# Mirrored rows of W: by a matmul with a flipped identity, or by a gather and sums on GpSimd

## The chip, the core and the metric

The kernel runs on one core of a Trainium2 chip. A core has five engines that work in parallel, each through its own instructions in their order: TensorE (PE: matrix products into PSUM), VectorE (DVE), ScalarE (ACT), GpSimd (POOL, which doesn't reach PSUM) and SyncE (SP, which here only issues DMAs). They wait for each other through semaphores. The metric is the device time of one execution in microseconds, lower is better.

## The reference

A transformer block with cross-attention and a Fourier layer, all in float32: `x` is (2, 2048, 512), the context (2, 128, 512).

```python
q = layernorm(x) @ wq + bq;  k = ctx @ wk + bk;  v = ctx @ wv + bv     # 16 heads of 32
score = (q . k) / sqrt(32) * mask;  score = where(score == 0, -1e9, score)
x = x + softmax(score) @ v @ wo + bo
w = complex(w_freq_real, w_freq_imag)                                  # (512, 512)
x = x + real(ifft(fft(layernorm(x)) @ w)) + bias
```

The Fourier layer is linear, so it equals `layernorm(x) @ M` with one real matrix M of 512x512. The kernel computes M once, on the chip, from the two halves of w and a table of cosines and sines. By symmetry the product needs only sums and differences of mirrored rows (row j of w with row 512 - j), then of mirrored columns.

## The kernel before

The 4096 rows of x are worked on in eight groups of 512 rows, each of four tiles of 128 rows. For a tile: scores of 16 heads (`scores`, PE), two softmax halves of eight heads (`Softmax`), transposes of the weights (`transposed_weights`, PE, copied out of PSUM by ACT or DVE). For a group: queries (`Queries`, four chains of four matmuls each), context, output projection, and the Fourier layer (`Ffn`) with M, which lies in `m_ffn`.

The order of all work is written out by hand. Each engine runs its instructions in the order in which the program names them; nothing is reordered. Groups 1 to 7 are made of `slot` calls (one tile of the last group excepted), one for a tile, each with three chains of matmuls. Group 0 is written out line by line, since there M is also made, between the tiles:

- `load_rows`, `load_residual` and `load_mask` put loads on SP's queue. wr and wi hold rows 1 to 256 (in `[:, :HC]`) and 256 to 511 (in `[:, HC:]`) of the two halves of w, by two DMAs each; row 0 lies in `row0`.
- `FoldRows` (four of them, two chunks of wr and two of wi): PE multiplies a chunk by `flip`, an identity with its columns reversed (L602), which gives the chunk with its rows mirrored in PSUM; DVE adds it to the upper half (L609) and subtracts it (L612), with small repairs of row 0 (L611, L614).
- `fold_columns` (L633, L634): POOL makes sums and differences of mirrored columns, into `cols`.
- `Mirrored`: `half` is made of `cols` and the table `dft` (L673), then `m_ffn` of `half`; ACT evicts each product (L683, L693) and POOL or DVE writes its mirrored other half (L694, L695). The first rows are added by `load_first_rows` (four small DMAs, `rows_h` and `rows_m`) and `first_rows`.

Two pools of PSUM matter for the order: `mm` has two buffers, through which all chains of four matmuls go (queries, values, flips, M), and `tp` has two, for transposes. A third chain can't begin before the first one's buffer is emptied.

A softmax half is, in the order of its steps: `masked` (DVE L328, reads PSUM and the mask), `maxima` (DVE L335, which reads its SBUF tile twice, L337, L338), `exponentials` (ACT, eight instructions of L344), `divided` (DVE L356, then POOL L357). The layer norm of the next groups' rows is spread between: `relative` (L228, subtracts a row's first element, on POOL, DVE or ACT), `query_statistics` (DVE L203 and L204, then POOL L207 and L208), `query_norm` (DVE L211), `query_transposes` (PE L186, evicted by ACT L188).

Of the kernel before, what the change touches and what calls it, by code (L numbers as in the profile page):

```python
# [14 lines left out]
P = 128  # L15
# [7 lines left out]
def kernel(  # L23
# [73 lines left out]
    ident = const_tile([P, P], "ident")  # L97
    make_identity(nc, ident)
    ctx.enter_context(tc.manual_schedule())
    flip = const_tile([P, P], "flip")  # L100
    nc.vector.tensor_copy(flip, ident[:, P - 1 :: -1])
    power = const_tile([P, TG], "power")
    nc.vector.memset(power, -0.5)

# [55 lines left out]
    row0 = const_tile([1, 2, D], "row0")  # L160
    nc.sync.dma_start(row0[:, 0, :], wf_re[0:1, :])
    nc.sync.dma_start(row0[:, 1, :], wf_im[0:1, :])
    nc.sync.dma_start(wr[:, :HC, :], chunks(wf_re[1 : HD + 1, :]))
    nc.sync.dma_start(wr[:, HC:, :], chunks(wf_re[HD:, :]))
    nc.sync.dma_start(wi[:, :HC, :], chunks(wf_im[1 : HD + 1, :]))
    nc.sync.dma_start(wi[:, HC:, :], chunks(wf_im[HD:, :]))
    nc.sync.dma_start(wv, chunks(wv_w))
    bv = const_tile([P, D], "bv")
    nc.sync.dma_start(bv, wv_b.partition_broadcast(P))
    dft = big_tile("pt", 6, "dft")  # L170
    nc.sync.dma_start(dft[:, :HC, :], chunks(dft_cos[HD:, :]))
    nc.sync.dma_start(dft[:, HC:, :], chunks(dft_sin[HD:, :]))
# [96 lines left out]
    class Queries:  # L269


        def __init__(self, i, g, first=0):
            self.i, self.g, self.first = i, g, first

        def pe(self):
            i, g = self.i, self.g
            if i not in qTs:
                qTs[i] = big_tile("qT", 2, f"qT_{i}")
            self.ps = chain(
                f"q_{i}_{g}",  # L280
                lambda c: wq[:, c, g * P : (g + 1) * P],
                lambda c: xnTs[i][:, c, self.first * P :],
                width=GQ - self.first * P,
            )

        def evict(self):
            nc.scalar.activation(  # L287
                qTs[self.i][:, self.g, self.first * P :],
                self.ps,
                AF.Identity,  # L290
                bias=bq[:, self.g : self.g + 1],
            )
# [290 lines left out]

    m_ffn = const_tile([P, NC, D], "m_ffn")
    half = big_tile("pt", 6, "half")
    cols = big.tile([P, 4, HC, HD], FP, tag="cT", bufs=1, name="cols")

    class FoldRows:  # L590

        def __init__(self, name, t, other, sign, c):
            self.name, self.t, self.other, self.sign = name, t, other, sign
            self.c = c

        def pe(self):

            t, c = self.t, self.c  # L600
            self.low = ps_mm.tile([P, D], FP, tag="mm", name=f"low_{self.name}_{c}")
            nc.tensor.matmul(  # L602
                self.low, flip, t[:, HC - 1 - c, :], start=True, stop=True
            )

        def evict(self):
            t, c = self.t, self.c
            total, high = t[:, HC - 1 - c, :], t[:, HC + c, :]
            nc.vector.tensor_tensor(total, self.low, high, ALU.add)  # L609
            if c == 0:  # L610
                nc.vector.tensor_copy(total[0:1, :], high[0:1, :])  # L611
            nc.vector.tensor_tensor(high, high, self.low, ALU.subtract)  # L612
            if c == 0:
                nc.vector.tensor_scalar(  # L614
                    high[0:1, :], row0[:, self.other, :], self.sign, None, ALU.mult
                )

        on_vector = True

    def fold_columns():  # L620


        up, down = slice(HD + 1, D), slice(HD - 1, 0, -1)
        rp, rm, ip, im = wr[:, :HC, :], wr[:, HC:, :], wi[:, :HC, :], wi[:, HC:, :]
        for k, (x1, x2, op, first) in enumerate(
            (
                (rp[:, :, up], rp[:, :, down], ALU.add, rp[:, :, HD : HD + 1]),
                (im[:, :, up], im[:, :, down], ALU.add, im[:, :, HD : HD + 1]),
                (ip[:, :, down], ip[:, :, up], ALU.subtract, rp[:, :, 0:1]),
                (rm[:, :, up], rm[:, :, down], ALU.subtract, im[:, :, 0:1]),  # L630
            )
        ):
            nc.gpsimd.tensor_tensor(cols[:, k, :, 1:], x1, x2, op)  # L633
            nc.gpsimd.tensor_copy(cols[:, k, :, 0:1], first)  # L634

    def cols_of(what, g):
        return lambda i: cols[
            :,
            2 * what + i // HC,
            HC - 1 - i if i < HC else i - HC,  # L640
            g * P : (g + 1) * P,
        ]

    def half_of(g):
        return lambda i: half[:, i, g * P : (g + 1) * P]
# [161 lines left out]
    for t in range(TG - 1):  # L807
        query_transposes(0, t)
    evict_keys()
    for t in range(TG):  # L810
        relative(1, t, nc.gpsimd if t < 2 else nc.vector)
    query_statistics(1, 0, TG - 1)
    for g in range(NC):
        first_queries(0, g)
    query_transposes(0, TG - 1)

    folds = [
        FoldRows(name, w, other, sign, c)  # L820
        for name, w, other, sign in (("wr", wr, 1, -1.0), ("wi", wi, 0, 1.0))
        for c in range(HC)
    ]
# [7 lines left out]
    m = [Mirrored(f"m_{g}", half_of(g), m_ffn[:, g, :], 1.0 / D) for g in range(NC)]  # L831
    rest = [Queries(0, g, 1) for g in range(NC)]
    q = [Queries(1, g) for g in range(NC)]

    w = begin(0, 0)
    w[0].masked()
    run(rest[0])
    w[0].maxima()
    query_statistics(1, TG - 1, TG)
    w[0].exponentials()  # L840
    w[1].masked()
    run(rest[1])
    run(rest[2])
    w[1].maxima()
    w[1].exponentials()
    run(rest[3])
    for t in range(TG):
        query_norm(1, t)
    w[0].divided()
    run(folds[0])  # L850
    w[1].divided()
    run(folds[1])

    load_rows(2)
    load_mask(1)
# [3 lines left out]
        query_transposes(1, t)  # L859
        relative(2, t, nc.gpsimd)  # L860
    w[0].maxima()
    values = [Values(b) for b in range(B)]
    values[0].pe()
    w[0].exponentials()
    w[1].masked()
    values[0].evict()
    transposed_weights(0, 0, 0, HC)
    w[1].maxima()
    values[1].pe()
    w[1].exponentials()  # L870
    transposed_weights(0, 0, HC, NC)
    values[1].evict()
    w[0].divided()
    run(folds[2])
    w[1].divided()
    run(folds[3])

    w = begin(0, 2)
    w[0].masked()
    fold_columns()  # L880
    rows_h = load_first_rows("rows_h", [x.lhs(HC)[0:1, :] for x in h])
    load_residual(0)
    w[0].maxima()
    run(q[0])
    transposed_weights(0, 1, 0, HC)
    w[0].exponentials()
    w[1].masked()
    query_statistics(2, 0, 2)
# [7 lines left out]
    w[1].divided()  # L896

    w = begin(0, 3)
    w[0].masked()
    q[2].evict()  # L900
# [5 lines left out]
    transposed_weights(0, 2, 0, HC)  # L906
    w[0].exponentials()
    w[1].masked()
    query_norm(2, 0)
    query_norm(2, 1)  # L910
    w[1].maxima()
    query_norm(2, 2)
    query_norm(2, 3)
    h[2].pe()
# [4 lines left out]
    transposed_weights(0, 2, HC, NC)  # L919
    w[1].exponentials()  # L920
    w[0].divided()
    run(q[3])
    m[0].pe()
    add = first_rows("add_m", rows_m, 1.0 / D)
    m[0].evict(add[:, 0:1])
    w[1].divided()

    q = [Queries(2, g) for g in range(NC)]
    load_rows(3)
    load_mask(2)  # L930
    w = begin(1, 0)
    w[0].masked()
    m[1].pe()
    m[1].evict(add[:, 1:2])
    w[0].maxima()
    w[1].masked()
    query_transposes(2, 0)
    query_transposes(2, 1)
    m[2].pe()
    m[2].evict(add[:, 2:3])  # L940
    query_transposes(2, 2)
    query_transposes(2, 3)
    for t in range(TG):
        relative(3, t, nc.gpsimd)
    w[0].exponentials()
    transposed_weights(0, 3, 0, HC, nc.vector)
    w[1].maxima()
    m[3].pe()
    m[3].evict(add[:, 3:4])
    transposed_weights(0, 3, HC, NC)  # L950
    q[0].pe()
    q[0].evict()
    w[1].exponentials()
    w[0].divided()
    query_statistics(3, 0, 2)
# [5 lines left out]
    for i in range(1, last - 1):  # L961
# [231 lines left out]
```

## Time and profile before

| | |
|---|---|
| median of 3 runs | 547.02 us (546.65 to 547.3) |
| profiled execution | 546.47 us, its span 544.7 us |
| PE | 528.8 us busy, 97% |
| DVE | 431.5 us busy, 79% |
| ACT | 342.9 us busy, 63% |
| POOL | 329.5 us busy, 61% |
| TensorE clock granted | 1.00 |
| DMA engines | 0.94 to 1.05 busy in the first 35 us, then 0.05 and less until 60 us |

The span is the time from the first to the last instruction on the core; the execution is 1.8 us longer. Lines such as L335 are lines of the kernel before. In the profile's lines of instructions the columns are: start in us, duration in us, engine, line, operation, tile written <- tiles read, shape, and `xN` where N equal instructions that follow each other are put together; in brackets the idle time of the engine before it, and what ended it.

### The profile page before, as it was taken

What the parts mean: (1) busy time and instruction counts of PE and PEld (TensorE: products, weight loads), DVE (VectorE), ACT (ScalarE), POOL (GpSimd) and SP (SyncE); (2) the same over time, 40 slices, a digit from 0 to 9 for tenths busy, and PEclk for the clock granted to TensorE, in tenths of its full rate; (3) what the DMA queues carried; (4) which work ended last, traced back from release to release, by engine and by line L of the source; (5) the groups of instructions that cost most, each with busy time, mean ns of one, the idle gap of its engine ahead of it and who ended that gap; (6) DMA issues with size and microseconds to landing.
All of it is one profiled execution on the core that took longest, in us unless ns stands there. A gap on an engine that the chain in (4) does not pass through costs nothing.

```text
span 544.7 us, 8783 instructions
## 1 busy us (share of the span) xinstructions
PE 528.8 (97%) x3005; PEld 292.7 (54%) x3005; DVE 431.5 (79%) x616; ACT 342.9 (63%) x1300; POOL 329.5 (61%) x268
## 2 busy tenths in 40 slices
PE   8989999999999999999999999999999999998997
PEld 7745566455545554455545555455545555554444
DVE  4798878899887989889887989889857898798251
ACT  3376886776677666666677676666686667756210
POOL 3256759826994469626895369626664466765450
PEclk9999999999999999999999999999999999999999
DMA  8950202000600024000510024000312001201102
GB/s 310 384 213 1 78 15 84 1 0 2 203 31 2 20 81 152 0 21 1 194 40 0 21 62 171 1 21 0 117 40 71 27 20 55 83 1 40 39 0 78
DMA packets 22992, 36.49 MB, mean 67 GB/s; under 512 B 2202, under 2 KB 6562, under 8 KB 22948
## 3 DMA queue, kind: packets, MB, share of 16 engines
q1 hardware_dynamic: 22260, 34.75, 18.4%
q10 hardware_dynamic: 688, 1.18, 0.6%
q8 instruction: 24, 0.39, 0.3%
q14 instruction: 20, 0.16, 0.1%
HBM read 27.53 MB, written 8.39 MB: 66 GB/s over the span
## 4 chain that ended last, share of the span: by engine, by line
PE 79%; DVE 11%; ACT 6%; POOL 1%; issue 1%; DMA 1%; SPq 0%; ACTq 0%; DVEq 0%; POOLq 0%
PE o L196 18%; PE y L196 17%; PE q L196 16%; PE tpw L370 8%; PE sc L309 5%; PE c L392 5%; ACT w L344 4%; DVE w L335 3%; DVE nmax L337 2%; PE tp_f L186 2%; DVE w L328 2%; PE tp_a L186 2%; PE k L535 1%; PE v L196 1%; DMA enc<-in_ctx_dram 1%
## 5 line engine op out<-in xcount | busy, mean ns | idle before, releaser
L344 ACT ACTIVATE w<-w,nmax 128x128 f32<-128x128 f32 x512 | 198.3, 395 | 19.2 <-DVE nmax L338 17.3
L357 POOL TENSOR_TENSOR w<-w,rden 128x1024 f32<-128x1024 f32 x64 | 123.7, 1933 | 120.0 <-DVE rden L356 59.9
L196 PE MATMUL o<-wo,cT 128*128 128x512 f32 x256 | 115.1, 594 | 0.0
L196 PE MATMUL y<-m_ffn,nT 128*128 128x512 f32 x248 | 112.4, 596 | 2.3 <-ACT nT L188 1.2
L196 PE MATMUL q<-xnT,wq 128*128 128x512 f32 (+1 forms) x256 | 112.0, 582 | 2.6 <-ACT qT L287 1.5
L377 ACT COPY pt<-tpw 128x512 f32<-128x512 f32 x122 | 65.6, 587 | 65.2 <-PE tpw L370 65.2
L344 ACT ACTIVATION_READ_ACCUMULATOR w<-w,nmax 128x1 f32 x512 | 99.4, 194 | 0.0
L335 DVE SCALAR_TENSOR_TENSOR w<-w 128x1024 f32<-128x1024 f32 x64 | 89.8, 1404 | 0.9
L328 DVE TENSOR_TENSOR w<-sc,mask 128x1024 f32<-128x1024 f32 x64 | 77.4, 1210 | 10.3 <-PE sc L309 9.9
L337 DVE TENSOR_REDUCE nmax<-w 128x8 f32<-128x1024 f32 x64 | 78.1, 1220 | 2.2
L370 PEld LDWEIGHTS tpw<-ident,w 128*128 128x128 f32 x512 | 59.4, 141 | 34.9 <-issue 29.3
L196 PEld LDWEIGHTS q<-xnT,wq 128*128 128x128 f32 x256 | 46.3, 190 | 48.6 <-issue 40.2
L196 PEld LDWEIGHTS o<-wo,cT 128*128 128x128 f32 x256 | 46.3, 190 | 47.9 <-issue 46.6
L196 PEld LDWEIGHTS y<-m_ffn,nT 128*128 128x128 f32 x248 | 44.7, 190 | 48.7 <-issue 44.8
L370 PE MATMUL tpw<-ident,w 128*128 128x128 f32 x512 | 67.9, 274 | 2.5 <-ACT nT L188 1.0
L447 POOL TENSOR_TENSOR x<-x,bf 128x512 f32<-128x512 f32 x32 | 48.9, 1528 | 18.3 <-DVE norm_f L211 18.3
L356 DVE RECIPROCAL rden<-den 128x8 f32<-128x8 f32 x64 | 12.7, 198 | 45.7 <-ACT w L344 45.7
L408 POOL TENSOR_TENSOR x<-x,bo 128x512 f32<-128x512 f32 x32 | 47.2, 1507 | 0.0
L309 PEld LDWEIGHTS sc<-kT,qT 32*128 32x128 f32 x1024 | 31.5, 186 | 21.0 <-issue 18.8
L228 POOL TENSOR_SCALAR rel<-rows 128x512 f32<-128x512 f32 x26 | 42.0, 1630 | 1.2 <-PE tp_a L186 1.2
L207 POOL TENSOR_SCALAR rstd_f<-mv_f 128x1 f32<-128x1 f32 x32 | 20.0, 625 | 34.8 <-DVE mv_f L204 34.8
L188 ACT COPY nT<-tp_f 128x512 f32<-128x512 f32 x30 | 17.1, 585 | 34.5 <-PE tp_f L186 34.4
(95 smaller groups left out, 535.1 us busy)
## 6 DMA issues: line engine op xcount, KB each, us to landing
rows<-in_x_dram SPq DMA_DIRECT2D x32, 256.0 KB, 4.7
x<-in_x_dram SPq DMA_DIRECT2D x32, 256.0 KB, 4.9
out_dram<-x SPq DMA_DIRECT2D x31, 256.0 KB, 2.0
mask<-in_mask_Bx1xSxS_fk_dram SPq DMA_DIRECT2D x8, 256.0 KB, 5.2
wk<-in_L_xattn_wk_w_dram ACTq DMA_DIRECT2D x2, 512.0 KB, 6.2
wq<-in_L_xattn_wq_w_dram SPq DMA_DIRECT2D x1, 1024.0 KB, 7.2
wr<-n_L_ffn_w_freq_real_dram SPq DMA_DIRECT2D x2, 512.0 KB, 5.2
wi<-n_L_ffn_w_freq_imag_dram SPq DMA_DIRECT2D x2, 512.0 KB, 7.7
```

The lines of the kernel that those rows point to most:

```text
L196: nc.tensor.matmul(ps, lhs(c), rhs(c), start=(c == 0), stop=(c == NC - 1))
L228: eng.tensor_scalar(d, xt, xt[:, 0:1], None, ALU.subtract)
L309: nc.tensor.matmul(sc[r // 2][:, r % 2, g, :], qTs[i][rows, g, t * P : (t + 1) * P], kT[rows, g, b * K : (b + 1) * K], start=True, stop=True,)
L328: nc.vector.tensor_tensor(self.w, self.sc.rearrange("p r g k -> p (r g) k"), self.mrow, ALU.mult)
L335: nc.vector.scalar_tensor_tensor(w, w, 0.0, w, ALU.is_equal, ALU.subtract)
L337: nc.vector.tensor_reduce(self.nmax, w, AX.X, ALU.min)
L344: nc.scalar.activation(w[:, h, :], w[:, h, :], AF.Exp, bias=self.nmax[:, h : h + 1], scale=-UNIT, accum_out=self.den[:, h : h + 1],)
L357: nc.gpsimd.tensor_tensor(w, w, rden.unsqueeze(2).to_broadcast([P, HH, K]), ALU.mult)
L370: nc.tensor.transpose(ps[:, r, :], ws[r // 2].w[:, (r % 2) * NC + g, :], ident)
L377: nc.scalar.copy(dst, ps)
L408: nc.gpsimd.tensor_tensor(xs[:, t, :], xs[:, t, :], bo, ALU.add)
L447: nc.gpsimd.tensor_tensor(xt, xt, bf, ALU.add)
```

## The change

The mirrored rows of w no longer come from PE. Four indirect DMAs on POOL's queue (two for wr, two for wi) gather rows 256, 255, ... 1 into the lower halves, with a list of row numbers that `iota` makes; the two plain DMAs that loaded the lower halves are gone. The sums and differences of mirrored rows are four POOL instructions over 128x1024 (`fold_rows`), into `half` and into the upper halves; the flips, `flip` and DVE's folds are gone. Row 0 is folded by itself on DVE (`fold_row0`), and `rows_h` is loaded from there, earlier. A factor of a half in the first row of `dft` (one DVE instruction on one row) replaces the repairs of row 0.

The order in group 0 is also changed. The first value chain stands in tile 0, where two flips were, the second stays in tile 1. The four query chains of group 1 stand in tiles 1 and 2 (before: 2 and 3), the first one of group 2 in tile 3, and its second in group 1's tile 0, so that group 1's tile 1 has two chains and not three. The last three chains of M are in group 1's tile 0, as before, and the first too. In tile 2 the copies of the first two transposes of weights now stand behind the first half's exponentials on ACT, in tile 3 they are DVE's. The fourth tile of group 1's rows is prepared later (`relative(1, TG - 1)`).

```diff
-    flip = const_tile([P, P], "flip")
-    nc.vector.tensor_copy(flip, ident[:, P - 1 :: -1])
+    mirror = const.tile([P, HC], mybir.dt.int32, tag="mirror", name="mirror")
+    nc.gpsimd.iota(mirror, pattern=[[-P, HC]], base=HD, channel_multiplier=-1)
...
-    nc.sync.dma_start(wr[:, :HC, :], chunks(wf_re[1 : HD + 1, :]))
     nc.sync.dma_start(wr[:, HC:, :], chunks(wf_re[HD:, :]))
-    nc.sync.dma_start(wi[:, :HC, :], chunks(wf_im[1 : HD + 1, :]))
     nc.sync.dma_start(wi[:, HC:, :], chunks(wf_im[HD:, :]))
...
+    def load_mirrored():
+        for t, rows in ((wr, wf_re), (wi, wf_im)):
+            for c in range(HC):
+                nc.gpsimd.indirect_dma_start(
+                    t[:, c, :],
+                    None,
+                    rows,
+                    bass.IndirectOffsetOnAxis(ap=mirror[:, c : c + 1], axis=0),
+                )
...
-    class FoldRows:
...
+    def fold_rows():
+        for k, t in enumerate((wr, wi)):
+            low, high = t[:, :HC, :], t[:, HC:, :]
+            nc.gpsimd.tensor_tensor(half[:, k * HC : (k + 1) * HC, :], low, high, ALU.add)
+            nc.gpsimd.tensor_tensor(high, high, low, ALU.subtract)
+    def fold_row0():
+        rows = const_tile([1, 2, HD], "fold0")
+        re, im = row0[:, 0, :], row0[:, 1, :]
+        nc.vector.tensor_tensor(rows[:, 0, 1:], re[:, up], re[:, down], ALU.add)
+        nc.vector.tensor_scalar(rows[:, 0, 0:1], re[:, HD : HD + 1], 2.0, None, ALU.mult)
+        nc.vector.tensor_tensor(rows[:, 1, 1:], im[:, down], im[:, up], ALU.subtract)
+        nc.vector.tensor_copy(rows[:, 1, 0:1], re[:, 0:1])
+        return load_first_rows(
+            "rows_h",
+            [rows[:, k, g * P : (g + 1) * P] for k in range(2) for g in range(HC)],
+        )
...
     evict_keys()
-    for t in range(TG):
+    load_mirrored()
+    for t in range(TG - 1):
         relative(1, t, nc.gpsimd if t < 2 else nc.vector)
-    query_statistics(1, 0, TG - 1)
+    query_statistics(1, 0, 2)
+    rows_h = fold_row0()
...
     w = begin(0, 0)
     w[0].masked()
+    fold_rows()
     run(rest[0])
     w[0].maxima()
-    query_statistics(1, TG - 1, TG)
     w[0].exponentials()
     w[1].masked()
     run(rest[1])
     run(rest[2])
     w[1].maxima()
     w[1].exponentials()
+    w[0].divided()
     run(rest[3])
+    relative(1, TG - 1, nc.vector)
+    query_statistics(1, 2, TG)
+    w[1].divided()
     for t in range(TG):
         query_norm(1, t)
-    w[0].divided()
-    run(folds[0])
-    w[1].divided()
-    run(folds[1])
+    run(values[0])
...
     w = begin(0, 2)
     w[0].masked()
     fold_columns()
-    rows_h = load_first_rows("rows_h", [x.lhs(HC)[0:1, :] for x in h])
+    nc.vector.tensor_scalar(dft[0:1, 0, :], dft[0:1, 0, :], 0.5, None, ALU.mult)
     load_residual(0)
+    run(q[1])
     w[0].maxima()
-    run(q[0])
-    transposed_weights(0, 1, 0, HC)
     w[0].exponentials()
     w[1].masked()
-    query_statistics(2, 0, 2)
+    transposed_weights(0, 1, 0, HC)
+    run(q[2])
     w[1].maxima()
-    run(q[1])
+    w[1].exponentials()
     transposed_weights(0, 1, HC, NC)
-    w[1].exponentials()
     w[0].divided()
     query_statistics(2, 2, TG)
-    q[2].pe()
+    query_norm(2, 0)
+    query_norm(2, 1)
+    run(q[3])
     w[1].divided()
...
         f_p = Ffn(p, 0)
-        second = q[1:]
+        second = [q[2], q[3], None]
```

More of the change, by code (lines that the diff above doesn't have):

```diff
@@ L588 @@
     cols = big.tile([P, 4, HC, HD], FP, tag="cT", bufs=1, name="cols")
-    class FoldRows:
[L594 to L618, printed above, removed]
+    def fold_rows():
[3 more added lines that the diff above has]
+            nc.gpsimd.tensor_tensor(high, high, low, ALU.subtract)
@@ new lines @@
+    up, down = slice(HD + 1, D), slice(HD - 1, 0, -1)
+    def fold_row0():
[9 more added lines that the diff above has]
+        )
@@ L620, in fold_columns @@
     def fold_columns():
-        up, down = slice(HD + 1, D), slice(HD - 1, 0, -1)
-        rp, rm, ip, im = wr[:, :HC, :], wr[:, HC:, :], wi[:, :HC, :], wi[:, HC:, :]
-        for k, (x1, x2, op, first) in enumerate(
-            (
[L627 to L630, printed above, removed]
+        rp, rm, ip, im = half[:, :HC, :], wr[:, HC:, :], half[:, HC:, :], wi[:, HC:, :]
@@ L631, in fold_columns @@
+        for k, (x1, x2, op, first, times) in enumerate(
+            (
+                (rp[:, :, up], rp[:, :, down], ALU.add, rp[:, :, HD : HD + 1], 2.0),
+                (im[:, :, up], im[:, :, down], ALU.add, im[:, :, HD : HD + 1], 2.0),
+                (ip[:, :, down], ip[:, :, up], ALU.subtract, rp[:, :, 0:1], 1.0),
+                (rm[:, :, up], rm[:, :, down], ALU.subtract, im[:, :, 0:1], 1.0),
             )
@@ L633, in fold_columns @@
             nc.gpsimd.tensor_tensor(cols[:, k, :, 1:], x1, x2, op)
-            nc.gpsimd.tensor_copy(cols[:, k, :, 0:1], first)
+            nc.gpsimd.tensor_scalar(cols[:, k, :, 0:1], first, times, None, ALU.mult)
     def cols_of(what, g):
[L637 to L642, printed above, removed]
+        return lambda i: cols[:, 2 * what + i // HC, i % HC, g * P : (g + 1) * P]
     def half_of(g):
@@ L815 @@
     query_transposes(0, TG - 1)
[L819 to L823, printed above, removed]
     h = [
@@ L833 @@
     q = [Queries(1, g) for g in range(NC)]
+    values = [Values(b) for b in range(B)]
     w = begin(0, 0)
     w[0].masked()
+    fold_rows()
     run(rest[0])
     w[0].maxima()
-    query_statistics(1, TG - 1, TG)
     w[0].exponentials()
@@ L861 @@
     w[0].maxima()
-    values = [Values(b) for b in range(B)]
-    values[0].pe()
+    transposed_weights(0, 0, 0, HC)
     w[0].exponentials()
     w[1].masked()
-    values[0].evict()
-    transposed_weights(0, 0, 0, HC)
+    values[1].pe()
     w[1].maxima()
-    values[1].pe()
+    transposed_weights(0, 0, HC, NC)
     w[1].exponentials()
-    transposed_weights(0, 0, HC, NC)
     values[1].evict()
     w[0].divided()
-    run(folds[2])
+    query_statistics(2, 0, 2)
+    run(q[0])
     w[1].divided()
-    run(folds[3])
     w = begin(0, 2)
@@ L880 @@
     fold_columns()
-    rows_h = load_first_rows("rows_h", [x.lhs(HC)[0:1, :] for x in h])
+    nc.vector.tensor_scalar(dft[0:1, 0, :], dft[0:1, 0, :], 0.5, None, ALU.mult)
     load_residual(0)
+    run(q[1])
     w[0].maxima()
-    run(q[0])
-    transposed_weights(0, 1, 0, HC)
     w[0].exponentials()
     w[1].masked()
-    query_statistics(2, 0, 2)
+    transposed_weights(0, 1, 0, HC)
+    run(q[2])
     w[1].maxima()
-    run(q[1])
+    w[1].exponentials()
     transposed_weights(0, 1, HC, NC)
-    w[1].exponentials()
     w[0].divided()
     query_statistics(2, 2, TG)
-    q[2].pe()
+    query_norm(2, 0)
+    query_norm(2, 1)
+    run(q[3])
     w[1].divided()
+    q = [Queries(2, g) for g in range(NC)]
     w = begin(0, 3)
     w[0].masked()
-    q[2].evict()
     w[0].maxima()
@@ L905 @@
         h[k].evict(add[:, k : k + 1])
-    transposed_weights(0, 2, 0, HC)
     w[0].exponentials()
     w[1].masked()
-    query_norm(2, 0)
-    query_norm(2, 1)
-    w[1].maxima()
+    transposed_weights(0, 2, 0, HC, nc.vector)
     query_norm(2, 2)
     query_norm(2, 3)
+    w[1].maxima()
     h[2].pe()
@@ L919 @@
     transposed_weights(0, 2, HC, NC)
+    for t in range(TG):
+        query_transposes(2, t)
     w[1].exponentials()
     w[0].divided()
[L922 to L925, printed above, removed]
+    run(q[0])
     w[1].divided()
-    q = [Queries(2, g) for g in range(NC)]
     load_rows(3)
@@ L932 @@
     w[0].masked()
+    m[0].pe()
+    add = first_rows("add_m", rows_m, 1.0 / D)
+    m[0].evict(add[:, 0:1])
     m[1].pe()
     m[1].evict(add[:, 1:2])
[L935 to L942, printed above, removed]
     for t in range(TG):
         relative(3, t, nc.gpsimd)
+    w[0].maxima()
     w[0].exponentials()
+    w[1].masked()
     transposed_weights(0, 3, 0, HC, nc.vector)
     w[1].maxima()
-    m[3].pe()
-    m[3].evict(add[:, 3:4])
+    for g in range(HC, NC):
+        m[g].pe()
+        m[g].evict(add[:, g : g + 1])
     transposed_weights(0, 3, HC, NC)
-    q[0].pe()
-    q[0].evict()
+    run(q[1])
     w[1].exponentials()
```

## The prediction

> **What bounds the kernel now.** I read the page's busy times first, then the waits of PE from 20 to 115 us (what is changed runs there), then the timelines of PE, DVE and POOL for the same stretch.
>
> ```profile
> PE 528.8 (97%) x3005; PEld 292.7 (54%) x3005; DVE 431.5 (79%) x616; ACT 342.9 (63%) x1300; POOL 329.5 (61%) x268
> ```
>
> PE is the bound: 97% busy, and from 100 us to 440 us nearly every step of the chain that ended last is a matmul. So a time lost or won on PE before 100 us reaches the end unchanged. PE's waits between 20 and 115 us are few (us in total, times, longest):
>
> ```profile
> PE q L196 <- ACT qT L287: 1.5, 1, 1.5
> PE q L196 <- ACT odd_half L693: 1.0, 1, 1.0
> PE low_wr L602 <- ACT qT L287: 0.9, 1, 0.9
> PE tpw L370 <- POOL m_ffn L695: 0.5, 1, 0.5
> ```
>
> PE's timeline (start, us):
>
> ```profile
> 21.15 8.01 PE L196 MATMUL q<-xnT,wq 128*128 128x384 f32 x24
> 30.63 2.85 PE L196 MATMUL q<-xnT,wq 128*128 128x384 f32 x8 [1.47 <-ACT qT L287]
> 33.32 1.02 PE L602 MATMUL low_wr<-wr,flip 128*128 128x512 f32 x2
> 35.28 1.12 PE L602 MATMUL low_wr<-wr,flip 128*128 128x512 f32 x2 [0.94 <-ACT qT L287]
> ...
> 113.07 1.09 PE L186 MATMUL tp_a<-ident,rel 128*128 128x128 f32 x8
> ```
>
> The fourth query chain (30.63) needs one of the two `mm` buffers, and ACT empties the second one only after the eight exponentials of the first softmax half, which wait for DVE's L338. DVE's timeline:
>
> ```profile
> 22.97 1.20 DVE L328 TENSOR_TENSOR w<-sc,mask 128x1024 f32<-128x1024 f32 x1
> ...
> 26.72 0.17 DVE L338 TENSOR_SCALAR nmax<-nmax 128x8 f32<-128x8 f32 x1
> ...
> 67.81 2.00 DVE L335 SCALAR_TENSOR_TENSOR w<-w 128x1024 f32<-128x1024 f32 x1
> ...
> 89.74 1.36 DVE L335 SCALAR_TENSOR_TENSOR w<-w 128x1024 f32<-128x1024 f32 x1
> ...
> 110.34 2.53 DVE L211 TENSOR_SCALAR rel<-rel,mv,rstd 128x512 f32<-128x512 f32 x2
> ```
>
> POOL's timeline, the first fence up to 115 us, the second from later:
>
> ```profile
> 13.00 0.72 POOL L208 TENSOR_TENSOR rstd<-rstd,power 128x1 f32<-128x1 f32 x1
> 14.89 3.30 POOL L228 TENSOR_SCALAR rel<-rows 128x512 f32<-128x512 f32 x2 [1.17 <-PE tp_a L186]
> ...
> 66.84 1.90 POOL L357 TENSOR_TENSOR w<-w,rden 128x1024 f32<-128x1024 f32 x1 [0.20 <-DVE rden L356]
> 68.69 1.71 POOL L694 TENSOR_TENSOR half<-half,odd_half 128x255 f32<-128x255 f32 x1
> ...
> 89.35 6.27 POOL L228 TENSOR_SCALAR rel<-rows 128x512 f32<-128x512 f32 x4
> ...
> 110.50 2.09 POOL L357 TENSOR_TENSOR w<-w,rden 128x1024 f32<-128x1024 f32 x1 [2.73 <-DVE rden L356]
> ```
>
> ```profile
> 159.92 1.28 POOL L408 TENSOR_TENSOR x<-x,bo 128x512 f32<-128x512 f32 x1
> ```
>
> Two facts carry the forecast. POOL is free from 18.2 to 27.8 us, where the new sums go. And DVE and POOL shut each other out: L335 with two SBUF inputs takes 1.22 us at 24.21, but 2.00 at 67.81, ending (69.81) 1.1 us after POOL's two-input L357 ends (68.74); then POOL's L694, 0.73 us elsewhere, takes 1.71 and ends just after it. So they alternate, a whole instruction each. Beside POOL's one-input L228 the same L335 takes 1.36 at 89.74: that one hardly shuts it out.
>
> **The change, part by part**
>
> *Removed from PE:* four flip matmuls of 0.86 us (a chain of four takes a pitch of 3.44): -3.4 us, all on the bound engine. Waits that go with them or with the new order, each with the 0.16 us by which a matmul outlasts its pitch (3.60 against 3.44): second flip 0.94, first q on wi 0.17, q on odd_half 0.96, tpw on m_ffn 0.53, and 0.5 + 0.3 inside `half` and before add_m: -4.0 us. DVE also loses eight tensor-tensors of 0.69 and four one-row instructions (0.61, 0.41), and gains five one-row ones (0.1 to 0.42) and two copies of 0.67: about 5 us less. DVE isn't what PE waits for in most of this, so I count no more for it.
>
> *Issuing the gathers.* Four indirect DMAs stand on POOL behind the last L208 (13.72) and ahead of the two L228. No row shows one. From below: SP's issues, 0.25 to 0.5 us; from above: a whole POOL pass over a tile, L357's 1.9 to 2.1. I take 1.1, by the nearest row of small POOL work on 128 rows (L208 at 128x4, 1.04). POOL then ends the two L228 at 13.7 + 4.4 + 3.2 = 21.3, not 18.2. DVE queues their statistics ahead of the first mask: done 22.1.
>
> *The sums.* Four POOL tensor-tensors 128x1024 with two full inputs: from L408 (1.28 for 512 columns) 2.5 each, 10 us; from below L357's 1.90. [...]
>
> When do they start? The gathers move 0.25 MB each while the DMA engines are full; wr's own 0.5 MB takes 5.2 us to land, so the first pair lands at 16 + 5 = 21, with POOL. Walk: sum 1 21.3-23.7. `fold_row0` on DVE has two instructions with two SBUF inputs, in front of the mask: the first waits to 23.7, sum 2 runs 24.1-26.6, the second waits for it, mask 26.9-28.1 (before: 22.97). Sum 3 27-29.4; L335 waits, 29.4-30.6; sum 4 30.6-33.1; L337, L338 waits, done 33.2 (before: 26.9). Exponentials 33.3-36.4, eviction 0.55, fourth q chain at 37.0 instead of 30.63: **+6.4 us of PE standing still**. The v chain put behind it (3.44) can't fill this: it stands after that q.
>
> *What is late next.* POOL's L357, the second group's rstd and the norms: ready by about 44, when PE has done q, v and scores (37.0 + 2.6 + 3.4 + 1.1): no gap. In tile (0,2) `fold_columns` (four sums of 1.1 to 1.3) meets DVE's L335, L338 and the new halving of dft, and the exponentials end at about 66.4. The evictions of the first tpw pair, ahead of those exponentials before, are now behind them in ACT's queue; PE comes for the third tpw at 56.4 + 3.44 + 0.87 + 3.44 = 64.2 and gets a buffer at 67.0: **+2.8**.
>
> *Four transposes in a row* in tile (0,3) go through two `tp` buffers at ACT's pace (0.55 a copy) behind two tpw copies: +1.2, bounds 0.5 and 2.
>
> *The moved q chain.* Group 1's tile 1 has two chains instead of three: 3.44 us of PE is done earlier, none removed. Norms on DVE (110.34, 2.53 us, held by L357) end at 112.87 and PE's tp_a starts at 113.07: 0.2 us of slack. PE comes 3.4 us sooner, DVE doesn't: **+3.2** waits there. From below zero, if DVE has itself been relieved.
>
> *At nothing:* `iota` (about 0.3 by the small POOL rows) delays `ident`, but PE only runs filler until 3.9 us. SP has two issues fewer; its four row copies for `rows_h` move ahead of the next rows and wait for DVE until 27; behind them rows of group 2 and a mask, the last row tile held by L228 on DVE until 37.6. It lands 4.7 us later and is read near 49: 7 us of cover.
>
> [...]
>
> *Sum:* -3.4 - 4.0 + 6.4 + 2.8 + 1.2 + 3.2 = **+6.2 us**. The profiled execution took 546.47 (span 544.7), so 552.7; the median of the runs is 0.55 above it: 553.2.
>
> **Rivals**
>
> 1. *No shutting out (faster).* If sums and DVE's instructions run side by side, the fourth q starts at about 31, nothing is late in (0,2), and half of the +3.2 goes: -3.4 - 4.0 + 0.1 + 1.2 + 1.4 = -4.7, 542.3. It decides if DVE's L335 beside a sum stays below 1.4 us. For it: L228 beside DVE. Against: 67.81, 110.34 and the mean of L335 (1.40 against 1.22). 12%.
> 2. *The rows land late,* at 25 or more. Then `fold_row0` and the mask escape, and the fourth q loses only 1 to 2 us, but the sums end at 36 to 38 and POOL's L357, rstd and so the norms of tile (0,1) are late by as much: net +4 to +7. 20%.
> 3. *Costly issue:* 2 us a gather puts 3.6 us more ahead of the statistics, all of it on the path: +10, 557. 17%.
> 4. *Cheap issue and sums* (0.3 and 1.9): L228 ends at 18.1, DVE runs as before, two sums are past before L335: +0.5 to +2.5, 549. 14%.
> 5. My own case: 37%.
>
> That the change doesn't do what it says isn't one: the flips are gone from PE's order.
>
> **The numbers.** The measurement can tell about 0.2%, 1.1 us. Faster: rival 1, 0.12. Same: the cheap end of rival 4, 0.04. Slower 0.84. The range leaves out rival 1 (12%) and of rival 3 what lies above 2.4 us a gather (8%): 547.8 to 558.5. Predicted is the likeliest case, 553.2.
>
> **What would show it.** Right: sums of about 2.5 us on POOL near 21 to 33 us; DVE's first mask near 27 and L335 and L338 beside sums inflated by 1 to 2 us; the fourth q chain near 37 after an idle of 7 or more; a PE wait on ACT in tile (0,2), and one on DVE's norms at group 1's tile 2. Wrong: L335 at 1.2 beside a sum, or the fourth q before 32 with no later wait; or a gap on POOL ahead of the gathers.

## The result, and the profile after

| | before | after |
|---|---|---|
| median of 4 runs | 547.11 us (546.65 to 547.3) | 557.12 us (555.98 to 557.27) |
| ratio | | 1.018 (95%: 1.0162 to 1.0197) |
| profiled execution, its span | 546.47, 544.7 us | 555.98, 554.1 us |
| mean granted TensorE clock | 1.00 | 0.988 |

The change makes the kernel 10 us slower, 1.8%. 553.2 was forecast, with a range of 547.8 to 558.5. In the kernel after, the lines of the helpers are ten higher: L345 is what was L335, L348 was L338, L206 was L196, L221 was L211, L238 was L228, L367 was L357.

Waits of PE from 20 to 130 us (us in total, times, longest):

```profile
PE q L206 <- ACT qT L297: 6.1, 1, 6.1
PE tp_a L196 <- DVE rel L221: 3.3, 2, 2.1
...
PE tpw L380 <- ACT pt L387: 0.2, 1, 0.2
```

PE's timeline, the places that answer to those shown of before:

```profile
21.25 8.01 PE L206 MATMUL q<-xnT,wq 128*128 128x384 f32 x24
35.31 5.18 PE L206 MATMUL q<-xnT,wq 128*128 128x384 f32 x8 [6.05 <-ACT qT L297]
...
118.29 0.84 PE L196 MATMUL tp_a<-ident,rel 128*128 128x128 f32 x4 [2.07 <-DVE rel L221]
120.33 1.09 PE L196 MATMUL tp_a<-ident,rel 128*128 128x128 f32 x4 [1.20 <-DVE rel L221]
121.21 5.68 PE L206 MATMUL o<-wo,cT 128*128 128x512 f32 x8
```

Two things are to be seen. The two long waits are the forecast ones: ahead of the fourth query chain (6.05 us, where 7 or more was forecast), and for the norms at group 1's tile 2. But the chain behind each of them is long as well: the same eight matmuls of the fourth query took 2.85 us before and take 5.18 here, and eight of `o` take 5.68 (granted clock 0.50 from 119 to 125) where they take 3.60 elsewhere. The reason stands in the column of the granted clock. Windows of 1 us: busy time and number of instructions of PE, PEld, DVE, ACT and POOL, then the granted clock, DMA share and GB/s:

```profile
32.00:33.00 1.00, 0.00 (x0) 0.00 (x0) 0.96 (x2) 1.00 (x7) 1.00 (x1) 1.00 0.23 82
33.00:34.00 1.00, 0.00 (x0) 0.00 (x0) 1.00 (x1) 1.00 (x7) 0.97 (x1) 0.62 0.76 266
...
39.00:40.00 1.00, 1.00 (x3) 0.40 (x3) 0.20 (x1) 0.73 (x4) 0.98 (x1) 0.50 0.91 278
40.00:41.00 1.00, 1.00 (x4) 0.58 (x3) 0.90 (x1) 0.47 (x1) 1.00 (x2) 0.97 0.01 2
```

PE's last matmul ended at 29.26. About 4 us later (a clock of 0.62 in the window from 33 means that it fell at 33.24) the clock is at one half, and it is back at 40.06 (0.97 in the window from 40), 6.8 us later. The forecast had no such term.

POOL's timeline, then DVE's:

```profile
13.89 1.50 POOL L173 DMA_INDIRECT wr<-n_L_ffn_w_freq_real_dram,mirror  x1 [0.20 <-issue]
...
18.20 0.95 POOL L173 DMA_INDIRECT wi<-n_L_ffn_w_freq_imag_dram,mirror  x1 [0.30 <-issue]
19.18 3.13 POOL L238 TENSOR_SCALAR rel<-rows 128x512 f32<-128x512 f32 x2
23.18 2.59 POOL L605 TENSOR_TENSOR half<-wr 128x1024 f32<-128x1024 f32 x1 [0.86 <-issue]
25.85 2.42 POOL L606 TENSOR_TENSOR wr<-wr 128x1024 f32<-128x1024 f32 x1
28.23 3.32 POOL L605 TENSOR_TENSOR half<-wi 128x1024 f32<-128x1024 f32 x1
31.62 2.35 POOL L606 TENSOR_TENSOR wi<-wi 128x1024 f32<-128x1024 f32 x1
```

```profile
20.81 0.70 DVE L213 BATCH_NORM_STATS2 st_a<-rel 128x6 f32<-128x512 f32 x1 [3.91 <-POOL rel L238]
...
23.55 2.50 DVE L617 TENSOR_TENSOR fold<-row 1x255 f32<-1x255 f32 x1
...
26.04 1.20 DVE L338 TENSOR_TENSOR w<-sc,mask 128x1024 f32<-128x1024 f32 x1
27.28 2.07 DVE L345 SCALAR_TENSOR_TENSOR w<-w 128x1024 f32<-128x1024 f32 x1
...
30.63 0.94 DVE L348 TENSOR_SCALAR nmax<-nmax 128x8 f32<-128x8 f32 x1
...
32.73 2.32 DVE L345 SCALAR_TENSOR_TENSOR w<-w 128x1024 f32<-128x1024 f32 x1
```

An instruction on one row of 255 elements takes 2.50 us because sum 1 is on the way (23.18 to 25.77): it ends just after it (26.05). L345 ends 1.1 us after sum 2 (28.27) and, the second time, 1.1 us after the fourth sum (33.97), and the third sum (3.32 instead of 2.42) stands back for the first L345. So the two engines do alternate. L348 is held as well (0.94 us, 0.17 elsewhere), though it reads only 128x8 elements. The mask, L338, isn't: it takes its 1.20 us beside sum 2.

### The profile page after: what moved, and what is told of

Same layout as the page of the kernel before. It is cut to its first block, busy times and chain, and to the rows that moved or that the text cites. A ratio compares the mean times of both kernels' runs of the same rounds, so it can differ in the third digit from the quotient of the medians.

```text
span 554.1 us, 8759 instructions
## 1 busy us (share of the span) xinstructions
PE 531.2 (96%) x2997; PEld 293.9 (53%) x2997; DVE 433.2 (78%) x610; ACT 342.2 (62%) x1298; POOL 347.6 (63%) x277
## 4 chain that ended last, share of the span: by engine, by line
PE 77%; DVE 11%; ACT 7%; POOL 3%; issue 1%; ACTq 0%; DVEq 0%; POOLq 0%
PE o L206 18%; PE y L206 17%; PE q L206 15%; PE tpw L380 8%; PE sc L319 5%; ACT w L354 4%; PE c L402 4%; DVE w L345 3%; PE tp_f L196 2%; DVE nmax L347 2%; PE tp_a L196 2%; DVE w L338 2%; PE k L545 1%; PE m L669 1%; POOL cols L634 1%; PE v L206 1%
## 5 line engine op out<-in xcount | busy, mean ns | idle before, releaser
L367 POOL TENSOR_TENSOR w<-w,rden 128x1024 f32<-128x1024 f32 x64 | 122.8, 1919 | 114.3 <-PE tpw L380 51.6
L206 PE MATMUL q<-xnT,wq 128*128 128x512 f32 (+1 forms) x256 | 114.4, 592 | 6.7 <-ACT qT L297 6.1
L206 PE MATMUL o<-wo,cT 128*128 128x512 f32 x256 | 117.2, 602 | 0.0
L206 PE MATMUL y<-m_ffn,nT 128*128 128x512 f32 x248 | 112.5, 596 | 2.3 <-ACT nT L198 1.2
L345 DVE SCALAR_TENSOR_TENSOR w<-w 128x1024 f32<-128x1024 f32 x64 | 91.0, 1422 | 0.9
L338 DVE TENSOR_TENSOR w<-sc,mask 128x1024 f32<-128x1024 f32 x64 | 77.5, 1212 | 10.8 <-PE sc L319 10.4
L347 DVE TENSOR_REDUCE nmax<-w 128x8 f32<-128x1024 f32 x64 | 78.1, 1220 | 2.2
L206 PEld LDWEIGHTS q<-xnT,wq 128*128 128x128 f32 x256 | 47.4, 194 | 53.7 <-issue 42.0
L206 PEld LDWEIGHTS o<-wo,cT 128*128 128x128 f32 x256 | 47.1, 194 | 49.3 <-issue 48.0
L206 PEld LDWEIGHTS y<-m_ffn,nT 128*128 128x128 f32 x248 | 44.7, 190 | 48.7 <-issue 44.8
L238 POOL TENSOR_SCALAR rel<-rows 128x512 f32<-128x512 f32 x26 | 43.5, 1686 | 3.8 <-PE tp_a L196 3.8
L319 PEld LDWEIGHTS sc<-kT,qT 32*128 32x128 f32 x1024 | 31.5, 186 | 21.2 <-issue 19.7
```

What stands on the lines that cost most here:

```text
L206: nc.tensor.matmul(ps, lhs(c), rhs(c), start=(c == 0), stop=(c == NC - 1))
L238: eng.tensor_scalar(d, xt, xt[:, 0:1], None, ALU.subtract)
L319: nc.tensor.matmul(sc[r // 2][:, r % 2, g, :], qTs[i][rows, g, t * P : (t + 1) * P], kT[rows, g, b * K : (b + 1) * K], start=True, stop=True,)
L338: nc.vector.tensor_tensor(self.w, self.sc.rearrange("p r g k -> p (r g) k"), self.mrow, ALU.mult)
L345: nc.vector.scalar_tensor_tensor(w, w, 0.0, w, ALU.is_equal, ALU.subtract)
L347: nc.vector.tensor_reduce(self.nmax, w, AX.X, ALU.min)
```

## The experiments

Gains against the kernel after are told as differences of the two distances to the kernel before that was run beside each (the kernel after: 10.0 us). Line numbers of helpers shift by a few between the kernels.

Theory A: the sums shut VectorE out of the first maxima, and with the late statistics this starves PE for some 6 us; an idle time of that kind also halves PE's clock for a while; the moved chain does the same again at 118 us. Against it: only the issue of the gathers counts, or the low clock has another cause, or the wait at 118 us is VectorE's and POOL's own.

**Is it the idle time that halves the clock?**

```diff
+    fill = ps_tp.tile([P, NC, P], FP, tag="tp", name="fill")
+    for k in range(44):
+        nc.tensor.transpose(fill[:, k % NC, :], ident, ident)
     run(rest[3])
```

> The changed kernel with 44 spare transposes of ident (into a tile that nobody reads) put on TensorE just ahead of the fourth first-tile query chain, where TensorE stood idle for 6.05 us; 44 at about 0.11 us fill 4.8 us of that idle time, so the chain cannot start earlier or later for it (35.3). Theory A (the idle time itself takes TensorE's clock to one half afterwards): granted clock 1.00 from 30 to 45, the chain of eight back at 2.85 us instead of 5.18, the span 2.3 us shorter, 554.8 us against 557.1. Theory B (the low clock between 33 and 40 has another cause, such as the load of GpSimd and VectorE at that time): clock 0.5 again, chain 5.2 us, 557 us, or later by what the filler itself then takes at half rate.

Median 555.04 us (552.6 to 555.93), ratio 1.0155 (1.0138 to 1.0172). The profiled execution is the one of 552.6, span 550.8, granted clock 1.000:

```profile
28.65 4.97 PE L843 MATMUL fill<-ident 128*128 128x128 f32 x44
36.85 2.85 PE L206 MATMUL q<-xnT,wq 128*128 128x384 f32 x8 [3.23 <-ACT qT L297]
```

The chain is back at 2.85 us, with the same sums beside VectorE in the first tile: the low clock follows the idle time. In this execution the clock stays up at 118 us too, though the waits there are the same (2.07 and 1.41). The other three runs had mean clocks of 0.994, 0.994 and 0.997 (3.4 us at half clock take 0.003 off the mean of this span), which is why the median gained 1.8 us and not more: 0.997 goes with 554.37 us, 0.994 with 555.70 and 555.93. The chain started 1.5 us later than in the kernel after, which was not expected: here both of `fold_row0`'s long instructions were caught by sums (2.11 and 2.50), there only the second (0.38 and 2.50).

**Do the sums alone do it, without gathers and late statistics?** The kernel before, and four sums, whose results are overwritten later:

```diff
     w[0].masked()
+    for t in (wr, wi):
+        low, high = t[:, :HC, :], t[:, HC:, :]
+        nc.gpsimd.tensor_tensor(half[:, :HC, :], low, high, ALU.add)
+        nc.gpsimd.tensor_tensor(half[:, HC:, :], high, low, ALU.subtract)
     run(rest[0])
```

> The kernel before, with nothing of the change but four GpSimd sums of 128x1024 (two reads of wr or wi each, written to half, whose content is overwritten later) queued where the changed kernel has its sums, between the first mask and the first maxima. No gather, statistics as early as before, flips as before. Theory A (GpSimd's two-input sums shut VectorE out of its one-input passes, which starves TensorE, whose clock then falls): L335 beside a sum about 2 us instead of 1.22, fourth query chain at 32 to 34 us instead of 30.63 and, if its idle time passes 4 us, at half clock; 550 to 554 us against 547.1. Rival (the gathers' issue ahead of the statistics is what costs, the sums are free beside VectorE): fourth chain at 30.6 to 31, 547 to 548 us.

550.89 us, ratio 1.0077 (1.006 to 1.0094). DVE's line, then PE's:

```profile
25.84 2.04 DVE L335 SCALAR_TENSOR_TENSOR w<-w 128x1024 f32<-128x1024 f32 x1
```

```profile
33.85 4.39 PE L196 MATMUL q<-xnT,wq 128*128 128x384 f32 x8 [4.44 <-ACT qT L287]
```

This is theory A: the fourth chain comes 3.2 us later than before, and at half clock for part of it (4.39 against 2.85; granted clock 0.65 from 33 to 35 and 0.80 from 35 to 40). L335 (2.04 instead of 1.22) makes only 0.8 us of the 3.2. As much comes from L338 (0.95 instead of 0.17), and the mask had already started 1.6 us later (24.59 against 22.97), as VectorE's L228 took 1.86 us beside a sum instead of 0.48. So instructions with one input are held too.

**The issue of the gathers ahead of the statistics:**

```diff
-    load_mirrored()
     for t in range(TG - 1):
         relative(1, t, nc.gpsimd if t < 2 else nc.vector)
+    load_mirrored()
```

> The changed kernel with the four gathers queued behind GpSimd's two relative rows instead of ahead of them. The statistics on VectorE end at about 18 us instead of 23.1, the mask then starts with the scores (about 21.5), and the gathers are issued from 17 to 22, so that the sums start some 3 us later (26 or later). Theory A (sums and late statistics each hold the first maxima back): the first exponentials start near 27 instead of 31.6, the second maxima still run beside sums; fourth chain at 32 to 34 instead of 35.3, part of the half clock left: 552 to 555.5 us. Rival (issue order alone): chain back at 30.6, full clock, 550 us. Rival (sums alone): no change, 557 us.

555.41 us, ratio 1.015 (1.0132 to 1.0168): 1.4 us less, though the whole loss of the first tile is gone (mask at 21.55, the four chains in one row from 21.45 to 32.09). It came back one step on. The sums now run to 37.5 on POOL, and what is queued behind them is late. DVE, then PE:

```profile
40.75 3.49 DVE L221 TENSOR_SCALAR rel<-rel,mv,rstd 128x512 f32<-128x512 f32 x4 [7.17 <-POOL rstd L218]
```

```profile
42.93 2.32 PE L196 MATMUL tp_a<-ident,rel 128*128 128x128 f32 x9 [6.31 <-DVE rel L221]
```

This is the form that rival 2 gave it: sums later, first tile spared, norms of the next group late. A wait of 6.05 us became one of 6.31, at half clock again behind it (0.61 between 40 and 45).

**The wait at 118 us: the eviction of the moved chain?**

```diff
-    run(q[1])
+    q[1].pe()
     w[1].exponentials()
+    q[1].evict()
```

> The changed kernel with the moved query chain q[1] of group 2 left where it is on TensorE (group 1, tile 0), but its eviction on ScalarE queued behind the second exponentials instead of ahead of them. TensorE's order is unchanged. Theory A (the chain's eviction holds ScalarE until TensorE has done the chain, so exponentials, reciprocal, masks and the norms of tile (1, 1) all come 4 us later): the two waits of tp_a on DVE rel (3.3 us) go, the granted clock between 118 and 126 stays 1.00, and the span falls by 3.3 + 2.1 = 5.4 us to 551.7. Rival (VectorE is late in tile (1, 1) because GpSimd's bias sums shut it out, whatever ScalarE does): waits of 3 us stay, 557 us. In between if another wait takes the place: 553 to 555.

557.5 us, ratio 1.0199 (1.0165 to 1.0232): no gain, and the waits are there (1.75 and 1.41). My mechanism, ScalarE held by the eviction, fell. VectorE isn't waiting for ScalarE there but for the context on PE, which stands behind the chain:

```profile
104.71 0.69 DVE L412 COPY cT<-c 128x512 f32<-128x512 f32 x1 [2.29 <-PE c L402]
```

The rival was that GpSimd's bias sums shut VectorE out. They do, but as much in the kernel before: beside them L345 takes 2.35 us in the kernel after (at 113.82), and L335 takes 2.36 in the kernel before (at 106.49).

**The chain itself moved back:**

```diff
-    run(q[1])
     w[1].exponentials()
...
-        second = [q[2], q[3], None]
+        second = q[1:]
```

> The changed kernel with query chain q[1] of group 2 moved back from group 1, tile 0 to tile 1, where the kernel before has it; nothing else. Theory A (in its new place the chain of 3.6 us stands on TensorE ahead of the context chains; VectorE's copies of them, which it does ahead of the masks of tile (1, 1), come 3.6 us later, and in tile (1, 1) TensorE has 3.6 us less to do while VectorE works): the waits of tp_a on DVE rel near 118 us (2.07 and 1.20 to 1.41) go, no low clock there, 3.3 to 5.4 us less than the changed kernel, 551.7 to 554 us. Rival (the norms are late since GpSimd's bias sums shut VectorE out in tile (1, 1), and would be late wherever the chain stands): the waits stay, 557 us.

555.03 us, ratio 1.0151 (1.0135 to 1.0167), 1.9 us less; 3.3 to 5.4 were expected. The waits on the norms are gone, and there is another in their place, of the same length (waits of PE, 20 to 130 us):

```profile
PE tpw L380 <- POOL w L367: 3.2, 2, 1.7
```

What was gained in the profiled execution is the second low stretch of the clock: here the clock has only the first one (mean 0.994, against 0.988 in the kernel after). From the scores of group 1's tile 0 to those of its tile 2 PE takes 31.2 us in the kernel before (80.76 to 111.97), 31.0 with the chain moved back (87.88 to 118.89), and in the kernel after 27.4 (87.68 to 115.05) and then the wait of 3.3. So these two tiles take 31 us in any of these orders. The change had already moved other work of PE ahead of them (the first chain of group 2 and its transposes), so PE had 3 us too little to do there, wherever q[1] stood.

**The sums later and on VectorE,** at the ends of tiles (0, 0) and (0, 1), two at each:

```diff
     w[0].masked()
-    fold_rows()
...
     run(values[0])
+    fold_rows(0, nc.vector)
+    fold_rows(1, nc.vector)
...
+    fold_rows(2, nc.vector)
     query_statistics(2, 0, 2)
     run(q[0])
     w[1].divided()
+    fold_rows(3, nc.vector)
```

> The changed kernel with its four sums of 128x1024 done by VectorE instead of GpSimd and later, at the ends of tiles (0, 0) and (0, 1), two at each, where the kernel before has its folds. Gathers, statistics and all else as in the changed kernel. Theory A (the sums beside the first maxima cost the first tile all but about 1 us of its loss): no L345 of the first tile over 1.3 us, the fourth query chain at 31 to 32 us instead of 35.3 to 37.1, no low clock between 33 and 40, norms not late; 5 to 6.5 us less than the changed kernel, 550.5 to 552 us. Rival (late statistics behind the gathers' issue are what costs): chain still at 34 or later, 555 us or more. Rival (the 4.9 us of added work on VectorE come back as a wait in tile (0, 1) or (0, 2)): 553 to 555.

553.57 us, ratio 1.0124 (1.0109 to 1.014), 3.3 us less; 5 to 6.5 were expected. PE:

```profile
31.52 4.54 PE L206 MATMUL q<-xnT,wq 128*128 128x384 f32 x8 [2.07 <-ACT qT L297]
...
63.93 1.14 PE L380 MATMUL tpw<-ident,w 128*128 128x128 f32 x8 [2.31 <-ACT pt L387]
```

The chain comes at 31.5 as theory A has it. Two things took part of the gain: even an idle time of 2.07 us was followed by a low stretch (granted clock 0.50 from 33 to 35, the chain 4.54), and now the wait of the third tpw in tile (0, 2), forecast at 2.8 and 0.15 in the kernel after, shows at 2.31, as PE comes there earlier (63.93 against 65.78). It had been hidden behind the first tile's loss.

**All three repairs together,** and the same with the late sums on GpSimd:

> Three edits of the changed kernel together: gathers queued behind the two relative rows on GpSimd, the four sums on VectorE at the ends of tiles (0, 0) and (0, 1), q[1] of group 2 back in tile (1, 1). If the losses of the changed kernel are those of theory A and no others, what stays is the removed flips and their waits: the fourth query chain at 30.6 to 31, clock 1.00 throughout, 1 to 5 us less than the kernel before, 542 to 546 us. If a further loss is hidden behind the ones removed: 547 to 550.

> As the kernel with all three edits, but with the four late sums on GpSimd instead of VectorE. Theory A (a two-input sum on GpSimd costs by what it shuts out beside it: each holds one L345 or mask of tile (0, 1) by about 1 us, and the relative rows and column sums queued behind the sums come 5 us later): 1 to 4 us more than with the sums on VectorE, 545 to 549 us. Rival (only the first tile is sensitive): within 0.5 us of the kernel with the sums on VectorE.

554.05 us, ratio 1.0125 (1.0107 to 1.0143), and 558.24 us, 1.0226 (1.02 to 1.0252). The first is 8 us above what was expected, and 4 above the case of a hidden loss. PE's waits between 50 and 110 us are those of the kernels above (2.31 for the third tpw, 1.73 and 1.42 for the divisions), and the first mask was late in a way that I can't explain:

```profile
24.14 1.22 DVE L338 TENSOR_TENSOR w<-sc,mask 128x1024 f32<-128x1024 f32 x1 [4.29 <-PE q L206]
```

The matmuls of its scores are recorded from 20.02 to 21.19, and VectorE had nothing else to do, yet their semaphore came at 24.1. The kernel with the sums on GpSimd shows the same; the one with only the gathers moved (mask at 21.55) does not. The second kernel shows that late sums on GpSimd cost 4.2 us more than on VectorE, slightly more than expected; PE's waits for divisions are 5.8 us there, against 4.1, and the mean granted clock of its profiled execution is 0.991, against 0.994.

**The gather alone, in the old order.** The kernel before with the flips replaced by gathers (behind the relative rows) and sums, values, queries and M's chains where they were:

```diff
     for t in range(TG):
         relative(1, t, nc.gpsimd if t < 2 else nc.vector)
+    load_mirrored()
     query_statistics(1, 0, TG - 1)
+    rows_h = fold_row0()
...
-    run(folds[0])
+    fold_rows(0, nc.vector)
     w[1].divided()
-    run(folds[1])
+    fold_rows(1, nc.vector)
```

and the same at the places of the third and fourth fold; the second kernel has all four sums on GpSimd behind the first mask, as the change has them.

> The kernel before with the gather alone: flips gone, four gathers queued behind GpSimd's two relative rows, the four sums of 128x1024 on VectorE at the four places of the former folds, row 0 by the four one-row operations and the halved row of the cosines as in the changed kernel; values, queries and matrix sums stay in the tiles of the kernel before. The earlier kernels with all repairs stayed at 554 us, with waits of tp_w on ScalarE in tile (0, 2) (2.3 us) and on GpSimd's divisions in tile (1, 1) (3.2 us). Theory A (those waits come from chains having been brought forward into tiles that are paced by VectorE and GpSimd, with nothing left for TensorE behind): with the old order they are gone and the flips' 3.4 us and 1 us of waits are gained, 541.5 to 545 us. Rival (VectorE and GpSimd pace these tiles in the old order too, so that TensorE's saved time returns as waits): 546 to 548 us. Rival (the gathers hold something in the first tile, as the mask that started at 24.1 instead of 21.5 in the repaired kernels would have it): 548 to 552 us.

> As the kernel with the gather alone, but the four sums on GpSimd between the first mask and the first maxima, as the changed kernel has them. With that kernel it gives the price of the sums' place and engine alone, and with the changed kernel the price of the new places of values, queries and matrix sums. Theory A: the sums start near 27.5 and hold the norms of group 1 (their deviations are queued behind the sums on GpSimd, till 39.7) and the second maxima: a wait of TensorE of 6 us near 37 and a stretch at half clock; 4 to 8 us more than with the sums on VectorE, 547 to 552 us, and 5 to 10 us less than the changed kernel. Rival (the new places cost nothing, all loss is the sums'): 555 to 558 us.

With the sums on VectorE 546.56 us, ratio 0.9996 (0.9987 to 1.0005): no difference from the kernel before. Theory A had 541.5 to 545, the first rival 546 to 548. With the sums on GpSimd 548.67 us, ratio 1.0032 (1.0021 to 1.0043). So the sums' engine and place cost 2.1 us in this order (4 to 8 were expected), and what else the change does (the new places, and the gathers ahead of the statistics) costs the remaining 8 us (1.018 against 1.0032 of 547). These 8 us hold the first tile's longer wait too, so they aren't the chains' alone.

Why does the gather alone gain nothing, with 3.4 us of flips gone? In its profile the fourth chain is at 31.52 and half slow (idle 2.24, 4.54 us; granted clock 0.50 from 32 to 35), since `fold_row0` put the mask 0.9 us back; that is 2.6 us. What is left of the gain, 0.8 us, is still there at the scores of group 1's tile 0 (79.98 against 80.76 before). Two kernels try to get this back.

```diff
     query_statistics(1, 0, TG - 1)
-    rows_h = fold_row0()
...
     fold_rows(3, nc.vector)
+    rows_h = fold_row0()
```

The second has the statistics of the last two row tiles behind the second maxima, too.

> As the kernel with the gather alone and its sums on VectorE, but the four one-row operations on row 0 moved from ahead of the first mask (where they took 0.8 us of VectorE, and the mask started at 23.85 instead of 22.97) to behind the last sum in tile (0, 1). If that 0.8 us made the fourth query chain's idle time 2.24 us and with it the stretch of 3.4 us at half clock: chain at 30.6 to 30.9 after 1.4 us of idle time, full clock, 2.6 us less, 543.5 to 544.5 us, faster than the kernel before by 0.4 to 0.6%. Rival (tiles (0, 1) to (0, 3) are paced by VectorE, so the time gained returns as waits there): 545.5 to 547 us.

> As the kernel with row 0 late, and with the statistics of group 1's last two row tiles (and the last relative rows) moved behind the second maxima of the first tile, where the changed kernel has them. The first mask can then start with the scores at 21.5, and the fourth query chain follows without idle time; against it the norms of group 1 come later, about 34.5 instead of 32, and TensorE waits some 2 us for them behind the scores of tile (0, 1). If the early chain and the late norms balance: within 1 us of the kernel with row 0 late. If the first mask starts at 24 all the same, as it did in the two repaired kernels, where the semaphore of the scores came 3 us after their records: chain at 31.5 or later at half clock, 546 to 548 us.

549.55 us, ratio 1.0054 (1.004 to 1.0068), and 550.91 us, 1.007 (1.0057 to 1.0084): both slower, and outside every case expected for them. PE with row 0 late:

```profile
30.62 2.85 PE L206 MATMUL q<-xnT,wq 128*128 128x384 f32 x8 [1.48 <-ACT qT L297]
...
67.91 1.99 PE L670 MATMUL half<-dft,cols 128*128 128x257 f32 x8 [2.72 <-ACT add_half L656]
```

The first tile is as in the kernel before, clock 1.00 throughout. Then the gain is lost: the one-row instructions, now beside a division and a column sum of GpSimd, take 2.10 and 1.42 us of VectorE ahead of tile (0, 2)'s mask (0.38 and 0.40 before the move), and waits of 1.04 (division), 0.91 (eviction of a query) and 2.72 (`add_half`) follow; the scores of group 1's tile 0 start at 82.00. So the move won 2.6 us in the first tile and lost 4.6 behind it. In these orders tiles (0, 1) to (0, 3) are paced by VectorE, GpSimd and ScalarE. But the new place of the one-row instructions is itself part of this loss, and a place where nothing of GpSimd runs beside them was not tried: what the gather alone could gain there stays open. The second kernel's mask started at 21.10, and its fourth chain didn't wait; 1.9 us of waits for ScalarE's copies and 1.6 for divisions came instead, and the wait of 2.72 stayed. No version is faster than the kernel before.

## Why the prediction was right, and where its steps were off

The direction and the mechanism hold; the median lies 3.9 us above the forecast and inside the range. That it is inside is partly luck: the room above 553.2 had been left for a costlier issue of the gathers, which didn't come, and the clock, which the forecast left out, filled most of it. The execution with the filler ran at full clock all through, and can be laid against the sum step by step, since the filler lies in time that PE stood idle: its span is 550.8, 6.1 above 544.7, where +6.2 was forecast.

- *First tile, +6.4.* With the filler +6.2 (36.85 against 30.63), and in the kernel with the late eviction +6.5 (37.11). In the profiled execution of the kernel after only +4.7: the first one-row instruction (0.38 us) got in ahead of sum 1, because the rows landed 0.86 us after POOL was free.
- *Flips and waits gone, -7.4.* I compare the times from the start of one group of matmuls to the start of the next, in the kernel before and in the filler's execution. 7.3 us are gone: 4.8 at the flips (3.4 of it their own), 0.25 at the first q on wi, 1.1 at q on odd_half, 0.7 at tpw on m_ffn, 0.4 inside `half`. Only the 0.3 before add_m isn't found. The term holds.
- *Third tpw, +2.8, transposes in a row, +1.2.* 3.4 us came instead of 4.0, but at other places: 0.4 at the third tpw (its wait was 0.15), 2.2 at the transposes (waits of 0.59, 0.19 and 0.68, with their tails), and 0.8 that was not forecast, 0.5 of it at the tpw behind group 1's transposes. That the sum comes out near is luck. From the start of the fourth chain to the scores of group 1's tile 2 it was 81.34 us before (30.63 to 111.97) and 77.41 with the filler (36.85 to 114.26): -3.9, where these terms make -3.4. That the wait of 2.8 exists is shown by 2.31 in the kernel with its sums on VectorE: another loss was in front of it.
- *The moved chain, +3.2.* The waits were 3.3 (3.5 with the filler), and the rest of the way to the first `o` chain makes it +3.7. But the reason was only half right. I said that VectorE wouldn't come sooner, and it doesn't: from the scores of group 1's tile 0 to the end of the norms it takes 32.1 us before (80.76 to 112.87) and 32.5 after (87.68 to 120.18). But with the chain moved back PE waits as long, for GpSimd. So it isn't this chain's place that costs; by the 31 us of these two tiles in each order, it is that work was brought forward out of them.
- *Issue, 1.1 a gather.* 1.25 from one to the next, the first 1.8; the four took 5.3 us, not 4.4. POOL's L238 ended at 22.3, not 21.3.
- *Sums, 2.5 each.* 2.34 to 2.62 where no whole tile of VectorE came between (2.59, 2.42, 2.35 in the kernel after). The row of L408 was a good guide.
- *What was missing:* the clock. Two low stretches cost 5.18 - 2.85 = 2.3 and 5.68 - 3.60 = 2.1 us in the profiled execution. With +4.7, -3.9 and, there, +4.1 for the moved chain that makes 9.3 of the 9.4 us by which the span grew. No row of before showed a low clock within the span (its mean is 1.00), but the forecast held an idle time of over 7 us, more than four times the longest that PE had there, and I took PE's speed after it for granted.

Of the rivals, the first is excluded (L345 at 2.07 and 2.32 beside a sum); rivals 3 and 4 too (1.25 us a gather, not 2 or 0.3); rival 2 did not come about in the kernel after (rows used from 23.2), but did when the gathers were moved back. None of the three signs of being wrong occurred. Of the signs of being right, two came short: the idle time ahead of the fourth chain was 6.05 us and not 7, and the wait on ScalarE in tile (0, 2) was 0.15 us. L345 and L348 were longer by 0.8 to 1.1 us beside a sum, at the low end of the 1 to 2.

## What to carry to other kernels

Where one engine is 97% busy, ask of every instruction that is taken off it which wait takes its place: here the 3.4 us of flips came back, in every order tried, as waits for engines that had been at 60 to 80%, and as half clock behind such waits. The two-input sums on GpSimd were paid for by VectorE's instructions beside them (0.8 to 1.1 us longer for both L345 and the first L348 in the kernel after, nothing for the mask), so put such a sum where nobody waits for VectorE, or give it to VectorE, whose own sum of this size took 1.17 to 1.25 us where it wasn't itself held by a division. And a forecast that has PE idle for about 2 us or more must allow for a slow stretch behind it: where one followed the wait ahead of the fourth chain (2.07 to 7.98 us), it cost that chain 1.5 to 2.6 us in these runs.

## What the runs showed of the hardware that I had not expected

- TensorE's granted clock fell to one half after idle times far shorter than the longest here, and not after every one of the same length. It fell after idle times of 2.07 us (sums on VectorE) and 2.24 us (gather alone), which cost 1.7 us on the chain behind each (4.54 against 2.85); it did not after 1.47 and 1.48 us, nor in the filler's execution after 3.23 us; and the pair of waits at 118 us brought a low stretch in the kernel after and none there. The wait of 2.72 us for `add_half` shows it at one place: the eight matmuls of `half` behind it took 2.68 us with the statistics moved (mean clock 0.996), and 1.99 with row 0 late (1.000). Which idle times bring the low clock is not shown. A low stretch lasted 3.4 us (gather alone, sums on VectorE) or 6.8 (both in the kernel after), and once, after an idle time of 7.98 us (late eviction), 10.2.
- VectorE's instructions on a single row were held like whole tiles: 1x255 with two inputs took 2.11 to 2.50 us beside a sum of 128x1024, 0.38 and 0.40 alone. Those on one element were not held (0.13), nor the mask, of whose two inputs one lies in PSUM (1.20), nor the reduction L347 (1.22). A one-input TENSOR_SCALAR was, even on 128x8 (0.94 to 1.86 us, 0.17 alone).
- A gather of 128 rows took GpSimd 0.95 us and 0.30 to the next, the first 1.25 or 1.50, and landed some 7 us after its issue (the median of a pair was 6.5 to 7.9 in five of the kernels; 7.7 and 7.0 in the kernel after, with the DMA engines 1.03 busy from 14 to 25 us). GpSimd stood idle for 0.20 us ahead of the first.
- In two kernels the semaphore of matmuls recorded as ended by 21.2 us reached VectorE at 24.1. What held it stays open.
